# Packing in halves, earlier covariances and unread products in a convolution and whitening kernel

## The chip, the cores and the metric

The kernel runs on one core of one Trainium2 chip. The metric is the device time of that core in microseconds (us), the median of several runs; lower is better. The core has TensorE (matrix products, PE in the profile; its weight loads are PEld), VectorE (DVE), ScalarE (ACT), GpSimd (POOL), SyncE (SP, which here only issues DMAs) and 16 DMA engines, which move data between the large memory (HBM) and the on-chip memory of 128 partitions. TensorE writes into PSUM, a small memory of eight banks, which VectorE and ScalarE empty.

## The reference

The input `x` has 4 images of 64 channels of 256 x 256 numbers in float32. Two layers are computed. The first convolves each channel with a filter of its own over the whole image, and adds `x` times a bias. The filter of a channel is the outer product of two one-dimensional filters, which a small network of sines makes:

```python
k = jnp.einsum('ijk,imk->ijmk', hx, hy)[0]
...
y = jnp.fft.irfft2(u_f * k_f, s=(fft_size, fft_size))[..., :L, :L]
out = y + x * bias[:, None, None]
```

The second layer whitens the 64 channels. The covariance comes from every ninth point, its inverse square root from five Newton-Schulz steps, and all points are multiplied by it:

```python
x1 = jnp.transpose(x, (1, 0, 2, 3)).reshape(B, -1)
x1_s = x1[:, ::STRIDE ** 2]
mean1 = jnp.mean(x1_s, axis=-1, keepdims=True)
xc = x1 - mean1
cov = x1_s @ x1_s.T / x1_s.shape[1] + EPS * jnp.eye(B, dtype=x.dtype)
deconv = _isqrt_newton_schulz(cov, N_ITER)
out = deconv @ xc
```

So no point of the output can be computed before every ninth point of all four convolved images has gone into one 64 x 64 matrix.

## The kernel before

Since a filter is an outer product, the convolution is two products with triangular Toeplitz matrices, one for each direction (L215). The work is cut into 32 steps. A step is one image `n` and one group `g` of 8 channels, and is walked in four groups of two channels, `c` = 0, 2, 4, 6. Steps 0 to 23 take channel groups 0 to 5, each for all four images; steps 24 to 31 take one image after another, with channel groups 6 and 7. Step 25 so ends image 0, step 27 image 1, step 29 image 2, step 31 image 3. "(27,4)" below is step 27, c=4.

`group(first, second)` (L384) computes the first direction of two channels and the second direction of the two channels that stood two groups earlier, in one interleaved stream of TensorE. ScalarE copies the first result (`o`, L399). VectorE adds bias times x to the second and leaves the convolved channels in the x tile (L402). The very first and the last two items are handled by `half_group` (L261).

Three things follow each group. `store(second)` (L410) writes the convolved channels to `y_d` in HBM (L415), and once a step, when the item with c=6 is done, appends nine packing operations to the list `todo`. One such operation (L314) is a predicated copy on VectorE of the points whose index fits the stride of nine, over both halves of the image, into the image's tile `samp[n]`. `pack(time)` (L378) takes operations from `todo` until their estimated cost has used up the time granted. In the last step a part of the channels is packed by TensorE instead (`pack_by_pe`, L289), with selection matrices.

`covariance(n)` (L322) multiplies the packed points of one image with themselves, 58 products of 65 columns on TensorE, and adds the result into `cov` on VectorE (L336). The covariances of images 0 to 2 stand between groups, at (27,4), (29,4) and (31,4); that of image 3 stands after the loop. `whitening` (L447) is a serial chain of small products on TensorE and small operations on VectorE and ScalarE; it contains `spin` products (L424), which nobody reads.

The last pass goes over 32 pieces of 4096 columns. A piece is read back from `y_d` (L352), multiplied by the whitening matrix (L616), shifted and moved out of PSUM by ScalarE (L621) and VectorE (L624), and written from GpSimd's queue (L629). The pieces have no tiles of their own: the list `homes` names, for thirteen pieces in turn, which pool's tile is taken over when its former user is done with it: Toeplitz tiles (t), packed tiles (s), x tiles (i), two spare ones (e). `load_next` issues the next load; the table `early` says after which groups of the loop it is called, and the rest is loaded after the last covariance. All loads and stores of the loop go through SyncE's queue in the order of the program text.

The order on each engine is the order of the program text (`tc.manual_schedule`); an instruction whose input is not ready holds up everything behind it on its engine. The lines that the prediction's steps touch are these:

- the loop over the steps, L553 to L580, with the place of `covariance` at L557
- `pack`, `group`, `store`: L378 to L420; the costs of packing operations: L316
- the end of the loop, L581 to L598: the last two `half_group`s with `pack(1.0)` each, `pack()` for what is left, the multiples of the identity `i15` (L590), `pack_by_pe`, the last covariance, the remaining loads, `whitening`

Of the kernel before, what the change touches and what calls it, by code (L numbers as in the profile page):

```python
# [40 lines left out]
ALU = mybir.AluOpType  # L41
# [3 lines left out]
NB, C, L = 4, 64, 256  # L45
# [3 lines left out]
CG = 8  # L49
# [16 lines left out]
def conv_whiten_kernel(ctx: ExitStack, tc: tile.TileContext, a: dict, out: bass.AP):  # L66
    nc = tc.nc
# [40 lines left out]
    steps = [(g, n) for g in range(C // CG - 2) for n in range(NB)]  # L108
# [10 lines left out]
    ident = const.tile([P, P], F32, tag="ident", name="ident")  # L119
# [33 lines left out]
    for i in range(3):  # L153
        for u in range(2):
# [3 lines left out]
            arg, k, nxt = (scratch[:, 2 + 3 * i + v, half] for v in range(3))  # L158
# [130 lines left out]
    def pack_by_pe(g, n, yt, cs):  # L289

        pk = psA.tile([P, H2, cs.stop - cs.start, NJ], F32, tag="psA", name=f"pk_{cs.start}")
        for s in range(STEP):
            for b in range(H2):
                nj = (L - s + STEP - 1) // STEP
                nc.tensor.matmul(  # L295
                    pk[:, b, :, 0:nj],
                    lhsT=pick[:, (s - b) % STEP, :],
                    rhs=yt[:, cs, b, s : s + STEP * (nj - 1) + 1 : STEP],
                    start=(s == 0 and b == 0),
                    stop=(s == STEP - 1 and b == H2 - 1),  # L300
                    skip_group_check=True,
                )
        dst = samp[n][:, :, :, g * CG + cs.start : g * CG + cs.stop]
        nc.scalar.copy(dst[:, 0], pk[:, 0].rearrange("p c j -> p j c"))  # L304
        copy = nc.vector.tensor_copy if cs.stop == CG else nc.scalar.copy
        copy(dst[:, 1], pk[:, 1].rearrange("p c j -> p j c"))

    def pack_ops(g, n, yt, cs):
        def op(s):
            nj = (L - s + STEP - 1) // STEP  # L310
            src = yt[:, cs, :, s : s + STEP * (nj - 1) + 1 : STEP].rearrange("p c b j -> p b j c")
            dst = samp[n][:, :, 0:nj, g * CG + cs.start : g * CG + cs.stop]
            m = mask[:, n, :, s : s + 1].unsqueeze(3).to_broadcast([P, H2, nj, cs.stop - cs.start])
            nc.vector.copy_predicated(dst, m, src)  # L314

        cost = 0.3 + 1.5e-3 * H2 * NJ * (cs.stop - cs.start)  # L316
        return [(cost, lambda s=s: op(s)) for s in range(STEP)]
# [4 lines left out]
    def covariance(n):  # L322

        pc = psA.tile([P, C + 1], F32, tag="psA", name=f"pc{n}")
        for b in range(H2):
            for j in range(NJ):
                half = slice(C * (j % 2), C * (j % 2 + 1))
                nc.tensor.matmul(  # L328
                    pc[half],
                    lhsT=samp[n][:, b, j, 0:C],  # L330
                    rhs=samp[n][:, b, j, :],
                    start=(b == 0 and j < 2),
                    stop=(b == H2 - 1 and j >= NJ - 2),
                    skip_group_check=True,
                )
        nc.vector.scalar_tensor_tensor(cov, pc, 1.0 / NSAMP, cov, ALU.mult, ALU.add)  # L336
# [4 lines left out]

    homes = [
        {"t": (tpool, "toep"), "s": (spool, "samp"), "i": (xpool, "in"), "e": (epool, "extra")}[k]
        for k in "eetssiistiits"
    ]

    def load_y(i):
# [7 lines left out]
    def load_next():  # L355
        loaded[len(loaded)] = load_y(len(loaded))

    loaded = {}
    todo = []
# [7 lines left out]
    for g in range(1, C // CG):  # L367
        first = 16 * g - 14 if g < C // CG - 1 else 16 * g - 22
        for part in range(8):
            k = first + (part * 12 // 8 if g < C // CG - 2 else part)  # L370
            blocks[k // 4, k % 4 * 2] = (g, part)

    early = {
        (26, 4): 1, (27, 0): 1, (27, 4): 1, (28, 0): 1, (29, 6): 1, (30, 2): 1, (31, 2): 1, (31, 4): 1, (31, 6): 1
    }
    orders = [list(range(L // HP)), list(reversed(range(L // HP)))]

    def pack(time=math.inf):  # L378
        while todo and time > 0:
            cost, op = todo.pop(0)  # L380
            op()
            time -= cost

    def group(first, second):  # L384

        units = []
        g1, n1, c1, x1, o1s1 = first
        g2, n2, c2, x2, o1s2 = second
        for u in range(2):
            job2 = (bank(f"p2_{g2}_{n2}_{c2 + u}"), o1s2[u], toep[g2][:, 1, c2 + u, :])  # L390
            job1 = (bank(f"p1_{g1}_{n1}_{c1 + u}"), x1[:, c1 + u], toep[g1][:, 0, c1 + u, :])
            units.append((job1, job2))

        toeplitz_products(units, orders[0])
        orders.reverse()
        for u in range(2):
            o1 = o1pool.tile([P, H2, L], F32, tag="o1", name=f"o1_{g1}_{n1}_{c1 + u}")
            for to, fr in ((slice(0, HP), slice(HP, P)), (slice(HP, P), slice(0, HP))):
                nc.scalar.copy(o1[to], units[u][0][0][fr])  # L399
            o1s1.append(o1)  # L400
            ch = g2 * CG + c2 + u
            nc.vector.scalar_tensor_tensor(  # L402
                x2[:, c2 + u], x2[:, c2 + u], bias[:, ch : ch + 1], units[u][1][0],
                ALU.mult, ALU.add,
            )

        pack(2.5)
        store(second)

    def store(second):  # L410
        g, n, c, yt, _ = second
        last = (g, n) == steps[-1]
        for b in range(H2):
            row = b * C + g * CG + c
            nc.sync.dma_start(  # L415
                out=y_d[n][row : row + 2, :].rearrange("c (p w) -> p c w", w=L),
                in_=yt[:, c : c + 2, b],
            )
        if last and c == CG // 2 - 2 or not last and c == CG - 2:
            todo.extend(pack_ops(g, n, yt, slice(0, c + 2)))  # L420

    spins = []

    def spin(times):  # L424

        p = psA.tile([P, P], F32, tag="psA", name=f"spin{len(spins)}")
        spins.append(p)
        for _ in range(times):
            nc.tensor.matmul(p, lhsT=ident, rhs=ident, start=True, stop=True)  # L429
# [113 lines left out]
    with tc.manual_schedule(  # L543
        engines={engines.PE, engines.SP, engines.DVE, engines.Activation, engines.Pool}
    ):
        toep = {0: new_toeplitz(0)}

        for f, lo, hi in ((0, 0, 2), (0, 2, 4), (0, 4, 6), (1, 0, 2), (0, 6, 8), (1, 2, 4), (1, 4, 8)):
            for half in range(2):
                load_toeplitz(toep[0], 0, f, half, lo, hi)  # L550
        for c in range(0, CG, 2):
            load_x(x_tiles[1], *steps[1], c)
        for i, (g, n) in enumerate(steps):  # L553
            xt = x_tiles[i % 4]
            for c in range(0, CG, 2):
                item = (g, n, c, xt, [])
                if g == C // CG - 1 and n > 0 and c == 4:  # L557
                    covariance(n - 1)
                if len(pending) == 2:
                    group(item, pending.pop(0))  # L560
                else:
                    half_group(item, 0)
                pending.append(item)
                if i == 0 and c == 6:

                    fold = const.tile([P, C], F32, tag="fold", name="fold")
                    nc.vector.tensor_tensor(fold, ident[:, 0:C], ident[:, C:P], ALU.add)

                    nc.scalar.activation(bf[:, 0:1], samp[0][:, 0, 0, C : C + 1], AF.Sqrt)

                if i + 2 < len(steps):
                    load_x(x_tiles[(i + 2) % 4], *steps[i + 2], c)
                if (i, c) in blocks:
                    tg, part = blocks[i, c]
                    if part == 0:
                        toep[tg] = new_toeplitz(tg)
                    lo = part % 2 * CG // 2
                    load_toeplitz(toep[tg], tg, part // 4, part // 2 % 2, lo, lo + CG // 2)
                for _ in range(early.get((i, c), 0)):
                    load_next()  # L580
        g, n, c, yt, _ = pending[0]  # L581
        for item in pending:
            half_group(item, 1)
            pack(1.0)
            store(item)

        pack()
        i15 = place(2 * C, rows=C).rearrange("p (u c) -> p u c", u=2)
        for u in range(2):
            nc.vector.tensor_scalar(i15[:, u], ident[0:C, 0:C], 1.5, None, ALU.mult)  # L590
        ones = place(P, rows=C)
        nc.gpsimd.memset(ones, 1.0)  # L592
        for lo in range(CG // 2, CG, 2):
            pack_by_pe(g, n, yt, slice(lo, lo + 2))
        covariance(NB - 1)
        while len(loaded) < len(homes):
            load_next()
        W, shift = whitening(i15, ones)  # L598


    halves = [slice(u * C, (u + 1) * C) for u in range(2)]
    for i, (n, q) in enumerate(pieces):
        yt = loaded.pop(i)
# [86 lines left out]
```

## Time and profile before

| | |
|---|---|
| median of 3 runs | 910.22 us (907.89 to 911.49) |
| the profiled execution | 911.4 us, its span 909.6 us |
| TensorE busy | 792.2 us, 87% of the span |
| VectorE busy | 657.6 us, 72% |
| ScalarE busy | 479.8 us, 53% |
| moved by DMA | 285.61 MB, mean 314 GB/s |
| products of L215, share of the chain that ended last | 64% |
| VectorE's L624 in the last pass, share of that chain | 13% |
| one L402 (128x512) | 743 ns, 252 of them |
| one packing copy L314, all channels of a group (128x448) | 972 ns |
| the same for half the channels (128x224) | 610 ns |
| one covariance on TensorE at full clock | 3.71 us |

The span counts from the first to the last instruction of the trace; the execution's time is 1.8 us more. Times in the trace are counted from the start of the span. The page cuts the span into 40 slices of 22.7 us and gives the busy share of each engine in tenths for each. A timeline lists instructions in order of time: start, duration, engine, line, operation, output and input tile, their shapes, how many, and in brackets how long the engine had been idle before and which instruction of which engine ended that. A window row gives the same engine's busy time between two times, with the clock that TensorE was granted (1.00 is full) and what the DMA engines did. A float32 product appears as two records.

The loads for the last pass are issued by SyncE at 510.54, 520.08, 531.15, 542.36, 576.53, 585.05, 603.36, 612.60 and 616.45 us in the loop, and the other four of the thirteen between 624.40 and 637.1.

### The profile page before, as it was taken

The page shows a single profiled execution, that of the slowest core. Times are in us where ns is not written, and L with a number is a line of the kernel's source. Part 1 is how long each engine was busy: PE and PEld are TensorE (multiplying, and loading weights), DVE is VectorE, ACT ScalarE, POOL GpSimd, SP SyncE. Part 2 cuts the span into 40 slices and gives each one's busy share as a digit, 9 for nine tenths or more (in the row PEclk, how much of TensorE's full clock was granted, in tenths as well). Part 3 has the DMA queues.
Part 4 walks back from the last instruction along what each step waited for, and adds up shares of the span by engine and source line. Part 5 has one row for each costly group of instructions (what it writes and reads, how often), then busy time and mean ns, then how long its engine had stood idle before and what let it go on. Part 6 is the DMA issues. An engine that isn't in the chain of part 4 may idle for free.

```text
span 909.6 us, 28286 instructions
## 1 busy us (share of the span) xinstructions
PE 792.2 (87%) x11928; PEld 636.7 (70%) x11928; DVE 657.6 (72%) x882; ACT 479.8 (53%) x798; POOL 31.4 (3%) x71
## 2 busy tenths in 40 slices
PE   8999999999999999999999999999977777775500
PEld 7999999999999999999999999998411111111100
DVE  3368786878687868876787766767699999996500
ACT  2545454545454545555555544541598888885400
POOL 3000000000000000000000000000110000000010
PEclk9999999999999999999999999998999999996655
DMA  4998788797888788878987898879899999999998
GB/s 154 303 305 261 250 243 263 251 276 247 253 262 265 247 255 267 263 249 253 297 282 234 285 400 323 290 253 386 346 383 433 428 432 429 428 433 428 432 430 342
DMA packets 117550, 285.61 MB, mean 314 GB/s; under 512 B 8973, under 2 KB 91312, under 8 KB 109744
## 3 DMA queue, kind: packets, MB, share of 16 engines
q1 hardware_dynamic: 110800, 216.49, 70.1%
q0 software_dynamic: 6336, 67.11, 17.4%
q8 instruction: 95, 1.56, 0.7%
q14 instruction: 31, 0.25, 0.1%
q10 hardware_dynamic: 288, 0.20, 0.1%
HBM read 149.35 MB, written 134.42 MB: 312 GB/s over the span
## 4 chain that ended last, share of the span: by engine, by line
PE 68%; DVE 15%; issue 14%; DMA 1%; POOL 0%; ACT 0%; POOLq 0%; SPq 0%; DVEq 0%; ACTq 0%
PE p L215 64%; DVE yi L624 13%; PE pc L328 2%; PE ph L247 1%; DVE samp L314 1%; PE busy L150 1%; POOL out_dram L629 0%; PE po L616 0%; DMA toep<-g_d 0%; DVE x L284 0%; PE spin L429 0%; PE pm L156 0%; DMA scratch<-in_zw_dram 0%; DMA g_d<-scratch 0%; DVE scratch L163 0%
## 5 line engine op out<-in xcount | busy, mean ns | idle before, releaser
L215 PE MATMUL p<-toep,x 64*64 64x64 f32 (+3 forms) x5040 | 578.5, 284 | 0.0
L215 PE MATMUL p<-toep,o 64*64 64x64 f32 (+3 forms) x5040 | 578.5, 284 | 0.0
L215 PEld LDWEIGHTS p<-toep,x 64*128 64x128 f32 (+1 forms) x5040 | 534.3, 166 | 23.4 <-issue 0.3
L215 PEld LDWEIGHTS p<-toep,o 64*128 64x128 f32 (+1 forms) x5040 | 535.2, 166 | 10.3
L399 ACT COPY o<-p 64x512 f32<-64x512 f32 x504 | 292.2, 580 | 296.0 <-PE p L215 288.5
L314 DVE COPY_PREDICATED samp<-mask,x 128x448 f32<-128x448 int32 (+3 forms) x288 | 281.0, 976 | 6.7
L402 DVE SCALAR_TENSOR_TENSOR x<-x,bias,p 128x512 f32<-128x512 f32 x252 | 177.3, 743 | 138.9 <-PE p L215 138.5
L624 DVE TENSOR_SCALAR yi<-po,shift 64x512 f32<-64x512 f32 x256 | 192.1, 750 | 22.2 <-PE po L616 16.0
L616 PE MATMUL po<-yi,chain 64*64 64x512 f32 x1024 | 152.7, 668 | 59.9 <-DVE yi L624 41.7
L621 ACT ACTIVATE yi<-po,shift 64x512 f32<-64x512 f32 x256 | 174.8, 683 | 38.9 <-PE po L616 31.4
L616 PEld LDWEIGHTS po<-yi,chain 64*64 64x64 f32 x1024 | 35.9, 145 | 175.7 <-DVE yi L624 129.6
L629 POOL DMA_DIRECT2D out_dram<-yi x44 | 23.6, 537 | 256.0 <-DVE yi L624 155.0
L592 POOL MEMSET chain<- 64x128 f32 x1 | 0.2, 198 | 603.0 <-PE ph L247 603.0
L328 PE MATMUL pc<-samp 128*64 128x65 f32 x464 | 17.3, 243 | 2.0 <-ACT samp L304 2.0
L328 PEld LDWEIGHTS pc<-samp 128*64 128x64 f32 x464 | 16.8, 155 | 3.2 <-ACT samp L304 2.2
L150 PE MATMUL busy<-idle 128*128 128x128 f32 x88 | 12.3, 304 | 0.0
L150 PEld LDWEIGHTS busy<-idle 128*128 128x128 f32 x88 | 11.9, 219 | 0.2 <-issue 0.2
L336 DVE SCALAR_TENSOR_TENSOR cov<-pc,cov 128x65 f32<-128x65 f32 x4 | 0.9, 226 | 14.7 <-PE pc L328 14.7
L281 DVE COPY o<-ph 64x256 f32<-64x256 f32 x8 | 3.4, 422 | 9.5 <-PE ph L247 9.4
L281 ACT COPY o<-ph 64x256 f32<-64x256 f32 x8 | 2.9, 366 | 10.4 <-PE ph L247 10.3
L295 PE MATMUL pk<-x,pick 128*128 128x56 f32 (+1 forms) x72 | 8.3, 292 | 0.0
L295 PEld LDWEIGHTS pk<-x,pick 128*128 128x128 f32 x72 | 8.1, 192 | 0.1
(92 smaller groups left out, 84.4 us busy)
## 6 DMA issues: line engine op xcount, KB each, us to landing
x<-in_x_dram SPq DMA_DIRECT2D x128, 512.0 KB, 5.6
y_d<-x SPq DMA_DIRECT2D x256, 256.0 KB, 4.2
yi<-y_d SPq DMA_DIRECT2D x32, 2048.0 KB, 15.1
out_dram<-yi POOLq DMA_DIRECT2D x28, 2048.0 KB, 43.2
out_dram<-yi POOLq DMA_DIRECT2D x16, 512.0 KB, 9.5
toep<-g_d SPq DMA_DIRECT2D x29, 256.0 KB, 6.4
toep<-g_d SPq DMA_DIRECT2D x29, 192.0 KB, 6.4
toep<-g_d SPq DMA_DIRECT2D x6, 128.0 KB, 3.0
```

The lines of the kernel that those rows point to most:

```text
L150: nc.tensor.matmul(p, lhsT=idle[:, 0:P], rhs=idle[:, P : 2 * P], start=True, stop=True)
L215: mm = nc.tensor.matmul(ps[q : q + w, m, HP * k : L], lhsT=src[parts, k // 2, m * P + q : m * P + q + w], rhs=t[parts, : stop : -1] if k e ...
L247: mm = nc.tensor.matmul(ps[m][:, HP * k : L], lhsT=src[parts, k // 2, m * P : (m + 1) * P], rhs=t[parts, : stop : -1] if k else t[parts, : ...
L295: nc.tensor.matmul(pk[:, b, :, 0:nj], lhsT=pick[:, (s - b) % STEP, :], rhs=yt[:, cs, b, s : s + STEP * (nj - 1) + 1 : STEP], start=(s == 0 ...
L314: nc.vector.copy_predicated(dst, m, src)
L328: nc.tensor.matmul(pc[half], lhsT=samp[n][:, b, j, 0:C], rhs=samp[n][:, b, j, :], start=(b == 0 and j < 2), stop=(b == H2 - 1 and j >= NJ ...
L399: nc.scalar.copy(o1[to], units[u][0][0][fr])
L402: nc.vector.scalar_tensor_tensor(x2[:, c2 + u], x2[:, c2 + u], bias[:, ch : ch + 1], units[u][1][0], ALU.mult, ALU.add,)
L616: nc.tensor.matmul(po[u][halves[k]], lhsT=W[halves[u]], rhs=yt[halves[u], cols[k]], start=True, stop=True,)
L621: nc.scalar.activation(yt[halves[0], cols[k]], po[0][halves[k]], AF.Identity, bias=shift[halves[k]])
L624: nc.vector.tensor_scalar(yt[halves[1], cols[k]], po[1][halves[k]], shift[halves[k]], None, ALU.add)
L629: nc.gpsimd.dma_start(out=o[:, end - part : end], in_=yt[:, end - part : end])
```

## The change

```diff
@@ homes
-        for k in "eetssiistiits"
+        for k in "eetssiistitis"
@@ early
-        (26, 4): 1, (27, 0): 1, (27, 4): 1, (28, 0): 1, (29, 6): 1, (30, 2): 1, (31, 2): 1, (31, 4): 1, (31, 6): 1
+        (26, 4): 1, (27, 0): 1, (27, 4): 1, (28, 0): 1, (29, 0): 1, (29, 6): 1, (30, 6): 1, (31, 0): 1, (31, 2): 1, (31, 6): 1
@@ pack
+    credit = [0.0]
+
     def pack(time=math.inf):
-        while todo and time > 0:
+        credit[0] += time
+        while todo and credit[0] > 0:
             cost, op = todo.pop(0)
             op()
-            time -= cost
+            credit[0] -= cost
+        if not todo:
+            credit[0] = min(credit[0], 0.0)
@@ group
-        pack(2.5)
         store(second)
+        pack(2.92)
@@ store
-        last = (g, n) == steps[-1]
+        halves = g >= C // CG - 2
...
-        if last and c == CG // 2 - 2 or not last and c == CG - 2:
-            todo.extend(pack_ops(g, n, yt, slice(0, c + 2)))
+
+        if c == CG - 2 and (g, n) != steps[-1]:
+            todo.extend(pack_ops(g, n, yt, slice(CG // 2 if halves else 0, CG)))
+        elif c == CG // 2 - 2 and halves:
+            todo.extend(pack_ops(g, n, yt, slice(0, CG // 2)))
@@ the loop over the steps
-                if g == C // CG - 1 and n > 0 and c == 4:
+                if g == C // CG - 1 and n > 0 and c == 0:
                     covariance(n - 1)
@@ the end of the loop
-            nc.vector.tensor_scalar(i15[:, u], ident[0:C, 0:C], 1.5, None, ALU.mult)
+            nc.gpsimd.tensor_scalar(i15[:, u], ident[0:C, 0:C], 1.5, None, ALU.mult)
...
             pack_by_pe(g, n, yt, slice(lo, lo + 2))
+        spin(4)
         covariance(NB - 1)
```

In steps 24 to 31 the eight channels of a step are packed in two parts of nine copies each, the first appended when the item with c=2 is done and the second when that with c=6 is done. The store now stands ahead of the packing, so that what it appends can be packed in the same group. The time granted for packing is 2.92 a group instead of 2.5, and what an operation overdraws is carried to the next group; what is not used is dropped when the list is empty. The first three covariances stand at (27,0), (29,0) and (31,0), two groups earlier. Ten loads instead of nine are issued in the loop, the fifth and later ones mostly earlier, and the eleventh and twelfth piece swap their homes (a Toeplitz tile and an x tile). Two operations of `i15` go from VectorE to GpSimd. Four products that nobody reads stand ahead of the last covariance.

## The prediction

> **What bounds the kernel now.** I read the page's slices first.
>
> ```profile
> PE   8999999999999999999999999999977777775500
> ...
> DVE  3368786878687868876787766767699999996500
> ...
> PEclk9999999999999999999999999998999999996655
> DMA  4998788797888788878987898879899999999998
> GB/s 154 303 305 261 250 243 263 251 276 247 253 262 265 247 255 267 263 249 253 297 282 234 285 400 323 290 253 386 346 383 433 428 432 429 428 433 428 432 430 342
> ```
>
> Each digit covers 22.7 us. Up to slice 27 (614 us) TensorE is full: the Toeplitz products of L215 set the pace, at 18.33 us for one step of four groups. After slice 29 (660 us) the DMA engines are full at about 430 GB/s: 19 pieces of 2 MB are still to be read and all 32 written. Between the two lies a serial tail, 614 to 651 us: last half groups, packing by TensorE, the last covariance, whitening, first output (issued at 650.90). Thirteen pieces can be loaded ahead, and in the trace all had landed when the first output was issued, for DMA idles at 649.25 to 652. So the bytes left at that point are fixed, and whatever moves the first output moves the end, one for one. Two places count: a stall of TensorE before 614, and the tail.
>
> The next view is VectorE's timeline around the first covariance.
>
> ```profile
> 506.09 1.41 DVE L402 SCALAR_TENSOR_TENSOR x<-x,bias,p 128x512 f32<-128x512 f32 x2 [3.53 <-PE p L215]
> 507.41 3.09 DVE L314 COPY_PREDICATED samp<-mask,x 128x464 f32<-128x464 int32 x3
> 510.41 1.40 DVE L402 SCALAR_TENSOR_TENSOR x<-x,bias,p 128x512 f32<-128x512 f32 x2
> 511.73 3.02 DVE L314 COPY_PREDICATED samp<-mask,x 128x464 f32<-128x464 int32 x3
> 515.27 1.41 DVE L402 SCALAR_TENSOR_TENSOR x<-x,bias,p 128x512 f32<-128x512 f32 x2 [0.52 <-PE p L215]
> 516.59 2.98 DVE L314 COPY_PREDICATED samp<-mask,x 128x448 f32<-128x448 int32 x3
> 519.50 1.39 DVE L402 SCALAR_TENSOR_TENSOR x<-x,bias,p 128x512 f32<-128x512 f32 x2
> 523.81 0.23 DVE L336 SCALAR_TENSOR_TENSOR cov<-pc,cov 128x65 f32<-128x65 f32 x1 [2.92 <-PE pc L328]
> ```
>
> The covariance of image 0 starts on TensorE at 520.05, ahead of group (step 27, c=4). Counting back, the L402 pairs at 519.50, 515.27, 510.41 and 506.09 belong to groups (27,2), (27,0), (26,6), (26,4). The nine packing copies of image 0's last channel group lie in (26,4), (26,6), (27,0), end at 519.57, and TensorE arrives 0.48 us later. Group (27,2) packs nothing; that one group is the cover.
>
> **The covariances moved by two groups.** I ran through the packing list as the new code fills and empties it. A full copy costs 0.996 in its account, a half copy 0.648. In step 24 three groups are filled by step 23's nine full copies, and only (24,6) appends step 24's first half, behind the last three full ones. From there on 18 half copies a step come in (11.664) against four grants of 2.92 (11.68): what is left over, 0.016 a step, never works off the queue that stands there. So a half appended at (i,2) waits behind four copies of the other half, and is packed in (i,4), five copies, and (i,6), four. For step 25 that is (26,4) and (26,6). The covariance now stands ahead of (27,0), directly behind (26,6). Steps 27 and 29, for the covariances at (29,0) and (31,0), give the same counts.
>
> What TensorE then waits for: VectorE must first do the two L402 of (26,6), which need that group's products, then four copies. No row shows a half copy in the loop; the tail has them, 0.66 us from start to start with 232 elements and 0.645 with 224:
>
> ```profile
> 624.40 0.63 DVE L314 COPY_PREDICATED samp<-mask,x 128x232 f32<-128x232 int32 x1
> ...
> 625.07 0.63 DVE L314 COPY_PREDICATED samp<-mask,x 128x232 f32<-128x232 int32 x1
> ```
>
> On the old times: L402 of (26,4) at 506.09, 1.32 us, five copies 3.3, so L402 of (26,6) at 510.7; plus 1.32, plus four copies of 224 (2.55) gives 514.6. TensorE ends (26,6) at 510.90 (ScalarE's copy of it starts at 510.14, and from such a copy, at 519.29, to the covariance it was 0.76). **Wait: 3.7 us, three times, 11.1 us.** Below, 3.1 each, if L402 of (26,6) starts when its bank is ready (510.1); above, 4.3, if VectorE lags by another half copy. Behind the waiting covariance on TensorE stand all later groups. VectorE's own L336 waits for it too, which costs nothing, since VectorE is idle then. Nothing fills these gaps: the new unread products stand only ahead of the last covariance.
>
> **The clock after such a wait.** The rows to weigh are the last covariance's, beside one in the loop, and the clock in quarter microseconds.
>
> ```profile
> 561.00 3.71 PE L328 MATMUL pc<-samp 128*64 128x65 f32 x116
> ...
> 620.55 8.28 PE L295 MATMUL pk<-x,pick 128*128 128x58 f32 x72
> 630.86 6.20 PE L328 MATMUL pc<-samp 128*64 128x65 f32 x116 [2.04 <-ACT samp L304]
> ```
>
> ```profile
> 629.25:629.50 0.25, 0.00 (x0) 0.92 1.73 594
> 629.50:629.75 0.25, 0.00 (x0) 0.50 1.07 373
> ...
> 636.00:636.25 0.25, 0.25 (x10) 0.50 0.77 328
> 636.25:636.50 0.25, 0.25 (x14) 0.92 1.52 590
> ```
>
> The columns after TensorE's busy time are the granted clock, DMA share and GB/s. After 2.04 us of idling the same 116 products take 6.20 instead of 3.71, at half clock from about 629.45 to 636.27. A second drop runs from 646.5 to 649.9. The edges fit a grid of 3.41 us. The Trainium skill (TensorE: Matmul & The Clock Gate, Part 1: The HAM clock gate) has the same free-running window of about 3.4 us, but lets the clock fall only after at least one idle window. By that rule the gap of 2.04 would have cost nothing, and a gap of 3.7 us holds a whole idle window in only (3.7 - 3.41)/3.41, some 8% of the phases: the clock mostly stays, and the three waits cost 11.1. By the row, 2.04 us suffices, and a window busy for its last 2.0 us (to 632.86) did not bring the clock back. I take the row: after each wait the work runs at half clock until the first window that is nearly all busy ends, 2.5 to 6.8 us later depending on phase. Half of that is lost, 1.2 to 3.4, about 2.2 in the mean; the row itself lost 2.5. **Three times 2.2 is 6.6 us**; bounds 0 (the rule) and 10.
>
> **The tail.** Before, VectorE packed until 630.25 although TensorE's own packing ended at 628.83 (the L295 row), and the covariance started at 630.86. In the new list (31,6) packs step 30's last four half copies; all nine of step 31's first half follow in the tail, two and one behind the half groups' own work and six at the end. On the old times: L402 of (31,6) 614.4 to 615.7, four copies to 618.3, L284 to 620.0, two copies to 621.3, L284 to 622.9, seven copies to 627.5. That is under TensorE's 628.83, so packing by TensorE is late next. Four unread products follow, eight passes at 0.117 (14 take 1.83 in whitening, 0.30 of it the first): to 629.77. The copies out of the last packing bank need about 0.6 and lie beside them. Then the covariance at full clock, 3.75 from its start to L336 (561.00 to 564.75): 633.5 instead of 637.10. **Minus 3.6 us.** If the clock fell anyway it is minus 1.1. The unread products cost some 0.5 over starting at once, and cover the gap in which the clock fell.
>
> **Costed at nothing.** Moving the 1.5 multiples of the identity to GpSimd: two small operations (its 128x128 one took 0.62) at about 620, used at 640.8; bare, they would delay whitening by under 1. Twice as many packing copies in steps 24 to 30: VectorE has 4 x 1.32 + 18 x 0.655 = 17.1 of 18.33 us a step, under TensorE; each bank of PSUM has one group's time to be emptied, so a lag of a few tenths stays hidden. Packing one group sooner in the first 24 steps: it frees x tiles that are loaded two steps ahead; SyncE's waits for it (49.2 us in all) were under TensorE too. Loads sooner and one more of them ahead of the loop's end: SyncE issues each in 0.4 to 0.8 us, and stores queue behind it. At (29,6) and (30,6) it waits for copies of the same group, some 2.6 us, and the stores behind it are late; but no x load comes after step 29, so TensorE doesn't see it. Swapped homes 10 and 11: SyncE takes the Toeplitz tile, free at 620.6, ahead of the x tile, free after 628.83. The thirteenth, freed by the last covariance at 633.5 instead of 637.1, lands within the 13 us to the first output as it did before, so that gains nothing. If they were late, a piece that is used thirteenth would be waited for, far behind the first output.
>
> **Sum**, against the profiled execution (span 909.6, time 911.4): +11.1 + 6.6 - 3.6 = +14.1, span 923.7, time 925.5. That execution lies 1.2 above the median of 910.22; on the median it is 924.3. I take 925.
>
> **Rivals.** (1) The waits come, the clock holds through them, as the skill's rule has it: 911.4 + 11.1 - 3.6 = 918.9. For it: products before and after are dense. Against: both drops in the trace. (2) On the other side: image 0's packing is complete before (26,6), because the queue is shorter there than I count. It decides from one group sooner: TensorE's 4.57 us a group then cover the 3.7, all three waits vanish, and only the tail's gain is left: 911.4 - 3.6 = 907.8. For it: (24,6) alone builds the queue, and without that group's backlog each half would be through in the group that appends it and the next, (26,2) and (26,4). Against: the account of costs leaves no way to work it off. (3) The edits to the tail don't do what they say (clock falls in spite of the unread products) and the waits cost the most: 911.4 + 12.9 + 10 - 1.1 = 933.2.
>
> **How the numbers follow.** Waits with clock loss 0.74, waits without 0.12, no waits 0.10, the costliest 0.04. The likeliest gives 925; within it 919 to 930. Down to 917 it takes in rival 1, and leaves out rival 2 and most of 3. A measurement can't tell 0.5% (4.6 us) from no change: rival 2 is half and half under 905.7 or over it, so faster 0.05, same 0.05, slower 0.90.
>
> **What would show it.** In the new trace: before each of the first three covariances TensorE idle some 3.7 us, released by VectorE's L314; granted clock 0.5 after it; a covariance or the group behind it longer by about 2. The last one at 3.7 instead of 6.2, with no idle ahead of it. First output some 14 us later, and the stretch from there to the end unchanged at 258.7 us. If the first three covariances have no idle ahead, I counted the list wrongly; if that last stretch shrinks, loads mattered where I gave them nothing.

## The result, and the profile after

The changed kernel takes 921.93 us in the median of 6 runs (920.60 to 926.08), the kernel before 909.82 beside it. The ratio is 1.0132, 95% interval 1.0113 to 1.0151: slower by 1.3%, where 925 was forecast, in a range of 917 to 930. The execution with the trace took 921.35, its span is 919.6.

Where the 10.0 us between the two spans lie can be read from five marks that both traces have: ScalarE's copy behind group (2,4), that behind the last group (31,6), the last L336, the issue of the first output, and the end.

| stretch | before | after | difference |
|---|---|---|---|
| start to group (2,4) | 66.59 | 67.24 | +0.65 |
| to the last group of the loop | 547.19 | 560.88 | +13.69 |
| to the last L336 | 23.32 | 19.66 | -3.66 |
| to the first output | 13.80 | 13.01 | -0.79 |
| to the end | 258.70 | 258.81 | +0.11 |

The loop lost 13.7 and the tail won 3.7. The first row is start-up: over the twelve traces of this study that mark lies between 65.9 and 68.8, so one execution can't tell a microsecond there. The row "to the first output" scatters with the clock: it takes 13.0 us in the five traces in which the granted clock stays full from the last L336 to the first output, and 13.8 to 15.5 in the seven in which it falls. The kernel before is one of the seven (0.50 from 646.5 to 649.9, as the prediction read), the changed one of the five.

The first view of the changed kernel is from its list of waits from 25 to 660 us: total, number, longest.

```profile
PEld pc L328 <- issue: 12.2, 3, 4.1
PE pc L328 <- DVE samp L314: 11.1, 3, 3.7
```

Before, TensorE waited for nothing ahead of the three covariances of the loop. The timelines of VectorE and of TensorE around the first one in the changed kernel:

```profile
506.95 1.40 DVE L407 SCALAR_TENSOR_TENSOR x<-x,bias,p 128x512 f32<-128x512 f32 x2 [0.81 <-PE p L215]
508.27 3.27 DVE L314 COPY_PREDICATED samp<-mask,x 128x232 f32<-128x232 int32 x5
511.43 1.39 DVE L407 SCALAR_TENSOR_TENSOR x<-x,bias,p 128x512 f32<-128x512 f32 x2
512.74 2.53 DVE L314 COPY_PREDICATED samp<-mask,x 128x224 f32<-128x224 int32 x4
520.79 0.23 DVE L336 SCALAR_TENSOR_TENSOR cov<-pc,cov 128x65 f32<-128x65 f32 x1 [5.52 <-PE pc L328]
```

```profile
515.42 5.26 PE L328 MATMUL pc<-samp 128*64 128x65 f32 x116 [3.69 <-DVE samp L314]
```

Five copies in one group and four in the next, then the covariance: TensorE had ended its products at 511.73 and waits until VectorE's fourth copy ends, near 515.3. (L407 is the former L402.) The covariance then takes 5.26 instead of 3.71. The window rows, with the granted clock behind TensorE's busy time, show why, and that it is not so each time. The first three are around the first covariance, the last two around the third:

```profile
516.00:516.25 0.25, 0.25 (x15) 0.88 2.12 655
516.25:516.50 0.25, 0.25 (x11) 0.50 0.95 262
...
519.50:519.75 0.25, 0.25 (x13) 0.80 0.91 320
...
604.75:605.00 0.25, 0.00 (x0) 1.00 0.15 53
...
606.75:607.00 0.25, 0.25 (x12) 1.00 0.00 0
```

The clock falls at 516.19 and comes back at 519.60. In the third wait, 602.95 to 606.6, it doesn't fall at all. In the tail the unread products close the gap:

```profile
642.99 1.10 PE L437 MATMUL spin<-ident 128*128 128x128 f32 x8
644.02 3.71 PE L328 MATMUL pc<-samp 128*64 128x65 f32 x116
```

### The profile page after: what moved, and what is told of

Its sections match the earlier page's. It is cut to its first block, busy times and chain, and to the rows that moved or that the text cites. A ratio compares the mean times of both kernels' runs of the same rounds, so it can differ in the third digit from the quotient of the medians.

```text
span 919.6 us, 28365 instructions
## 1 busy us (share of the span) xinstructions
PE 789.4 (86%) x11936; PEld 636.1 (69%) x11936; DVE 678.0 (74%) x943; ACT 479.9 (52%) x798; POOL 32.1 (3%) x73
## 4 chain that ended last, share of the span: by engine, by line
PE 67%; issue 14%; DVE 13%; DMA 4%; POOL 0%; POOLq 0%; ACT 0%; SPq 0%; DVEq 0%
PE p L215 61%; DVE yi L633 10%; DMA out_dram<-yi 2%; PE pc L328 2%; DVE samp L314 2%; DMA yi<-y_d 1%; PE ph L247 1%; DVE x L407 1%; PE pk L295 1%; PE busy L150 1%; POOL out_dram L638 0%; PE spin L437 0%; DMA toep<-g_d 0%; PE pm L156 0%; DMA scratch<-in_zw_dram 0%
## 5 line engine op out<-in xcount | busy, mean ns | idle before, releaser
L314 DVE COPY_PREDICATED samp<-mask,x 128x464 f32<-128x464 int32 (+3 forms) x351 | 296.8, 846 | 9.8 <-DMA y_d<-x 0.2
L407 DVE SCALAR_TENSOR_TENSOR x<-x,bias,p 128x512 f32<-128x512 f32 x252 | 179.1, 743 | 120.1 <-PE p L215 116.5
L625 PE MATMUL po<-yi,chain 64*64 64x512 f32 x1024 | 148.4, 649 | 63.2 <-DVE yi L633 42.2
L336 DVE SCALAR_TENSOR_TENSOR cov<-pc,cov 128x65 f32<-128x65 f32 x4 | 0.9, 227 | 18.6 <-PE pc L328 18.6
```

Of the source, the lines that this page charges most:

```text
L407: nc.vector.scalar_tensor_tensor(x2[:, c2 + u], x2[:, c2 + u], bias[:, ch : ch + 1], units[u][1][0], ALU.mult, ALU.add,)
L625: nc.tensor.matmul(po[u][halves[k]], lhsT=W[halves[u]], rhs=yt[halves[u], cols[k]], start=True, stop=True,)
```

## The experiments

Theory A was that the covariances wait for copies that stand in the queue ahead of them. The rival B was that the place of the covariances, the doubled number of copies or the earlier loads cost the time.

**The queue alone.** One number differs from the changed kernel: in steps 24 to 31 a group may spend 3.2 on packing.

```diff
-        pack(2.92)
+        pack(2.92 if g1 < C // CG - 2 else 3.2)
```

> The changed kernel with one number changed: in steps 24 to 31 a group is granted 3.2 for packing instead of 2.92. By the account the queue is then worked off in steps 24 to 26, the copies of image 0's last half end in (26,4), and those of images 1 and 2 in (28,4) and (30,4), one group before the covariances. Theory A (the covariance waits for copies that stand in its own group): no idle time ahead of the first three covariances, clock at full there, 11.1 + 2.4 us less than the changed kernel's 921.9, so 908.4, and 0.998 of the kernel before or a little less. Rival B (the place of the covariances, the doubled number of copies or the earlier loads cost the time, not the queue): no more than 2 us less than the changed kernel, 920 or over.

907.79 us (10 runs), ratio 0.9973 (0.9958 to 0.9989). VectorE and TensorE at the same place:

```profile
509.38 3.19 DVE L314 COPY_PREDICATED samp<-mask,x 128x224 f32<-128x224 int32 x5
512.47 1.39 DVE L407 SCALAR_TENSOR_TENSOR x<-x,bias,p 128x512 f32<-128x512 f32 x2
513.90 3.29 DVE L314 COPY_PREDICATED samp<-mask,x 128x232 f32<-128x232 int32 x5
```

```profile
512.80 3.71 PE L328 MATMUL pc<-samp 128*64 128x65 f32 x116
```

The copies ahead of the covariance end with image 0 (224 elements: the last five of nine); those behind 512.47 belong to the next image, and TensorE waits for none of them. From group (2,4) to the last group this trace takes 546.99, as before (547.19). All copies, places and loads are as in the changed kernel, so the whole loss of the loop is the queue. B falls. The margin is small: the copies end 0.23 us before the covariance starts.

**One group later instead.**

```diff
-                if g == C // CG - 1 and n > 0 and c == 0:
+                if g == C // CG - 1 and n > 0 and c == 2:
```

with the loads (29,0) and (31,0) moved to (29,2) and (31,2).

> The changed kernel with the first three covariances one group later, at (27,2), (29,2) and (31,2), and the two loads into their packed tiles moved with them, (29,0) to (29,2) and (31,0) to (31,2). The packing queue is as in the changed kernel. Theory A: the group between covers the four copies, no idle time ahead of the covariances, 908.4 as with the larger grant. Rival B (doubled copies or loads): 918 or over. If the copies of the group between delay the covariance as well, idle of up to 1 us each.

912.68 us (21 runs), 1.0029 (1.0019 to 1.0039). The wait for L314 is gone, as expected, but 4 us more are left than expected. In the trace TensorE pauses twice in a stream of products, for 1.93 and 1.06 us, which is 3.0 of the 4.0 us by which the loop is longer than with the grant of 3.2. The first pause:

```profile
523.63 0.27 PE L215 MATMUL p<-toep,o 64*128 64x128 f32 x1 [1.93 <-issue]
```

No releaser is shown. The DMA view of 521.0 to 521.5 has one packet (16 KB) on the queue of instructions, the first since 509.9:

```profile
q1 hardware_dynamic: 186, 0.18, 103.4%
q8 instruction: 1, 0.02, 11.8%
```

From 512.05 to its landing some 10 us later the 2 MB load of (26,4) was under way. Such packets usually come 4 to 9 us apart, but gaps of 11 us also stand in the trace of before (508.6 to 519.7) with no pause behind them. The next kernel leaves that load out (every load moves one place on the list):

> The kernel with the first three covariances at c=2, without the first load for the last pass at (26,4); every load moves to the next place of the list, nine stand in the loop. In that kernel's trace TensorE stood still for 1.93 us behind the covariance of image 0, with no releaser in the trace, and an instruction packet for TensorE's queue had come at 521.3, near the landing of the 2 MB load that was issued at 512.05, 12 us after the packet before it. Theory G (instruction fetch is held up behind such a load): no pause behind that covariance, 2 us less than 912.7 if no other load does the same elsewhere. Rival H (the pause belongs to the covariance's place, through a PSUM bank or VectorE): a pause of 1.9 us in the same place, and 912.7 again.

911.62 us, 1.0006 (0.9994 to 1.0018), where the one with the load had 1.0029. The pause at (27,2) is gone; one of 1.89 us now stands at 603.97, after a packet at 601.6 that came 11 us after its forerunner, with a load issued at 594.56. That speaks against the covariance's place and for an instruction packet that comes late. It doesn't settle it, nor that a load is what holds the packet up: long gaps without a pause exist, the two kernels were not timed side by side, and no run moved the packets alone.

**The clock's part.** Sixteen unread products ahead of each of the first three covariances (`spin(16)`):

> The changed kernel with sixteen unread products ahead of each of the first three covariances (32 passes at 0.117 us, 3.7 us each), which fill the wait and need nothing that is late. Measures the clock's part by itself. Theory A: the wait stays at 3.7 us less what the unread products overlap, so the covariance starts at the same time or at most 0.3 later, but all three take 3.7 at full clock; in the profiled execution that gives back the 2.4 us of clock loss, 1.5 to 3.5 in the median: 918.5 to 920.5. Rival C (the clock is no part of it, the loss lies in the waits alone): 921.9 or up to 1 over.

919.06 us (4 runs), 1.0097 (1.0077 to 1.0117), beside 1.0132: some 3 us. The two intervals just overlap, so it is the trace that carries this reading.

```profile
512.45 3.84 PE L437 MATMUL spin<-ident 128*128 128x128 f32 x32
516.22 3.71 PE L328 MATMUL pc<-samp 128*64 128x65 f32 x116
```

The wait is filled and not shortened, and the covariance takes 3.71. From group (2,4) to the last group the trace needs 558.20, 11.0 more than before: three waits of 3.7. So the clock's part of the changed kernel's 13.69 is 2.6 in its trace.

**Without the unread products of the tail.** The line `spin(4)` is taken out of the changed kernel.

> The changed kernel without the four unread products ahead of the last covariance. Theory A (they hold the clock over the gap in which the last packing bank is copied out): the covariance starts about 0.5 us sooner, after a gap of 0.4 to 0.6 us, and the clock falls as it fell in the kernel before after 0.6 us of idle in the window: 1.7 to 2.7 us lost, so 1.2 to 2.2 us over the changed kernel, 923.1 to 924.1. Rival D (so short a gap doesn't lower the clock): 0.5 us under it, 921.4.

923.15 us (5 runs), 1.0149 (1.0122 to 1.0176); the interval overlaps the changed kernel's. In the trace the last covariance starts after a gap of 0.31 us with the clock full, so the tail to L336 is 0.55 shorter (19.11), as the rival had it. The clock fell later, in whitening, so the stretch from L336 to the first output took 15.51 instead of 13.01; but it fell there in four traces that have the four products, too. The loop's part of the clock was 6.5 in this execution. What these four products are worth in the changed kernel stays open. In the kernel before they are worth something:

> The kernel before with four unread products ahead of the last covariance and nothing else. Theory A (the tail's 3.6 us are packing on VectorE first, 630.25 against 628.83, and clock second): the covariance starts at the same place, 0.9 of the 2.04 us gap are filled, and the clock falls later or not at all; between 0 and 2.5 us less than the kernel before. Rival (the unread products bring the whole 3.6 us): 3 us less or more.

909.24 us (22 runs), 0.9982 (0.9972 to 0.9993). The trace:

```profile
630.53 1.10 PE L429 MATMUL spin<-ident 128*128 128x128 f32 x8
632.71 3.71 PE L328 MATMUL pc<-samp 128*64 128x65 f32 x116 [1.07 <-ACT samp L304]
```

With half the gap filled the clock holds: 20.79 from the last group to L336, 2.53 under the kernel before. The ratio makes it less, 0.6 to 2.5 us; in this trace the clock fell between L336 and the first output, and gave back 0.9 there (14.69 against 13.80). What is left to the changed kernel's 19.66 is 1.13. It is the wait for the last copy of the packing, which the changed kernel does not have; there VectorE is done with its copies at 641.07, ahead of TensorE's own packing.

**The loads alone.** The changed kernel with the old table `early` and the old order of homes:

> The changed kernel with the loads for the last pass issued where the kernel before issued them, nine in the loop, and its order of homes. Theory A (the loads are no part of it, since all thirteen have landed when the first output is written): the changed kernel's 921.9 within 1 us, first output to end 258.7 to 259.1 as in all traces so far. Rival F (the tenth and earlier loads help, or their traffic is part of the loss): 2 us or more off it.

925.83 us (4 runs), 1.0161 (1.0135 to 1.0187): a miss, although this interval overlaps the changed kernel's. Its trace has 260.8 from first output to end where all others have 258.7 to 259.1. The window rows of 657 to 660, just before the first output (662.72 and 660.79), first this kernel, then the changed one; the number before last is the DMA share:

```profile
657.00:660.00 3.00, 2.62 (x22) 1.00 1.00 418
```

```profile
657.00:660.00 3.00, 2.63 (x25) 1.00 0.25 104
```

With the old table the loads are still under way when the first output is written, and the end is 2.0 us later. The last three of the thirteen loads are issued at 648.85, 649.24 and 649.82 here, and at 637.88, 645.14 and 647.82 in the changed kernel. (The two spans differ by 4.0 in all, since the clock's part in the loop is 5.1 in this trace and 2.6 in the other.) This run took back the table and the order of homes together, so it doesn't tell which of the two matters.

**A shorter tail, twice.** On top of the grant of 3.2, VectorE packs two channels more in the last step, TensorE two fewer:

```diff
             store(item)
+            if item[2] == CG - 4:
+                todo.extend(pack_ops(item[0], item[1], item[3], slice(CG // 2, CG // 2 + 2)))
...
-        for lo in range(CG // 2, CG, 2):
+        for lo in range(CG // 2 + 2, CG, 2):
             pack_by_pe(g, n, yt, slice(lo, lo + 2))
-        spin(4)
+        spin(14)
```

> The kernel with the grant of 3.2 and a shorter tail: in the last step VectorE packs two channels more (nine quarter copies, estimated at 0.47 us each from the full and half ones) and TensorE packs only the last two, 36 passes of 0.115 less; fourteen unread products instead of four hold the clock until VectorE is done. Theory A (the tail counts one for one): TensorE's packing ends 4.1 us sooner, VectorE's at about 629.8 on the old times, so the last covariance starts 1.3 us sooner: 906.5, 0.996 of the kernel before. Rival (something else sets the last covariance's start): 907.8 as with the grant alone.

913.61 us, 1.0032 (1.0015 to 1.0049): slower than with the grant alone.

```profile
622.95 7.39 PE L295 MATMUL pk<-x,pick 128*128 128x58 f32 x36 [1.98 <-DVE x L284]
630.15 5.23 PE L437 MATMUL spin<-ident 128*128 128x128 f32 x28
635.31 3.71 PE L328 MATMUL pc<-samp 128*64 128x65 f32 x116
```

With only the last two channels to pack, TensorE waits 1.98 us for them, the clock falls to 0.50 from 624 to 634, and packing and unread products run at half speed. VectorE was done at 628.97, so the unread products, meant as cover, had become the delay. The next kernel places nine ahead of the packing and eight behind it, in place of the fourteen:

> The kernel with the shorter tail, with its fourteen unread products split: nine ahead of TensorE's packing, where TensorE stood idle for 2.1 us and the clock fell, and eight behind it. Theory A (the idle time ahead of the packing let the clock fall, and the unread products behind it then ran at half clock and only delayed the covariance): full clock from the half groups to the last covariance, which starts about 15 us after the half groups began instead of 18.5, so 3.5 us less than that kernel, and 0.5 less than the one with the grant alone: 0.9968 of the kernel before. Rival (the shorter packing itself is slow, or the clock falls elsewhere): 1.000 or over.

907.75 us (10 runs), 0.9969 (0.9958 to 0.9980).

```profile
620.48 2.27 PE L437 MATMUL spin<-ident 128*128 128x128 f32 x18
622.59 4.36 PE L295 MATMUL pk<-x,pick 128*128 128x58 f32 x36
626.77 2.00 PE L437 MATMUL spin<-ident 128*128 128x128 f32 x16
628.98 3.71 PE L328 MATMUL pc<-samp 128*64 128x65 f32 x116 [0.21 <-ACT samp L304]
```

The same packing takes 4.36 instead of 7.39. The grant alone ran beside it:

> The kernel with the grant of 3.2 again, on the same chip as its successor, to compare the two. Theory A: 0.9973 of the kernel before, as it was, and no idle time of TensorE ahead of the first three covariances; a second profile also shows how far the clock's part scatters.

909.45 us (22 runs), 0.9986 (0.9977 to 0.9996), a little behind its first timing. The three waits for L314 are absent again, but the trace has one pause without a releaser of 1.86 us, in the second covariance. So the lowest ratio here belongs to the changed kernel with the grant of 3.2 and the shorter, warm tail: 0.3% under the kernel before and 1.6% under the changed one. Its trace shows the tail's gain (19.02 from the last group to L336 against 19.65), but the interval overlaps that of the grant alone, so between those two the times don't decide.

## Why the prediction was right

**The waits** were right in place, number and size: 3.69, 3.68 and 3.68 against 3.7 forecast, through five and four copies in the two groups ahead. The grant of 3.2 showed that it is the queue. (The covariance of the kernel before starts at 519.98, not at 520.05; that moves the forecast by 0.07.) The grant also brought about what rival 2 describes, a loop without waits, and ran in 907.79 where 907.8 had been worked out. That agreement is in part luck: the sum starts from the profiled execution, 1.2 above the median, and the same kernel took 909.45 the second time.

**The tail** was right: minus 3.66 against minus 3.6. Its parts in the traces, 2.53 from the clock and 1.13 from VectorE's packing, are those stated (2.5 and 1.1).

**The clock's term was too large**: 6.6 in the sum, 2.6 in the profiled execution, about 3 between the ratios with and without the filled waits. In the three traces with unfilled waits it was 2.6, 6.5 and 5.1. The step that failed was "after each wait the work runs at half clock until the first window that is nearly all busy ends", taken from the last covariance. The edges in the new trace, 516.19, 519.60, 560.56 and 563.97, are 1, 12 and 1 times 3.41 us apart. The rows show windows on that grid around the second and the third wait, with TensorE's busy time and the clock granted in the window:

```profile
557.15:560.56 3.41, 0.38 (x4) 1.00 0.94 357
560.56:563.97 3.41, 2.75 (x51) 0.50 1.06 399
...
601.52:604.93 3.41, 1.43 (x14) 1.00 0.16 53
604.93:608.34 3.41, 1.70 (x58) 1.00 0.82 231
```

The windows that ended in a drop were 11% busy here and 23% at the first wait. The two that share the third wait were 42% and 50% busy, and the clock stayed full. The window that brought it back after the second wait was 81% busy, short of "nearly all". So a wait of 3.7 us can cost nothing; here a window edge (604.93) fell in its middle. It did so once: in the three traces the clock fell in eight of nine such waits. No single busy share decides either. A window 38% busy ended in a drop in the kernel with the old loads, and one 45% busy in the kernel without the first load:

```profile
555.63:559.04 3.41, 1.30 (x14) 1.00 0.97 377
```

```profile
601.26:604.67 3.41, 1.52 (x27) 1.00 0.71 233
```

Of the two rules that were weighed, the Trainium skill's (TensorE: Matmul & The Clock Gate, Part 1: at least one idle window) asks for more idleness than these traces do. The row of the last covariance asks for less, since there the clock fell at the end of a window that packing by TensorE had kept 82% busy (2.79 us from 626.04 to 629.45). What is counted no run shows.

**"Gains nothing" for the loads** was half right. The new table and homes bring nothing over the old kernel's end stretch (258.81 against 258.70), but in the changed kernel they are needed: with the old ones the end comes 2.0 us later. I had compared the landing with the first output before, and not asked whether the old places would still be in time once the tail was 3.7 shorter. Whether they are needed without the waits in the loop no run shows.

The sum was +14.1 and the two spans differ by 10.0: minus 4.0 for the clock in the loop, minus 0.8 because the clock fell just ahead of the first output before and not after, plus 0.65 of start-up and small remainders. The time alone would not have told the forecast from rival 1: 921.93 lies about midway between 925 and the 918.9 of waits without clock loss. The traces tell them apart, and show a clock loss between the two.

## What to carry to other kernels

Where a list is filled at a rate equal to the rate at which it is emptied, whatever stands in it at the start stays. Run through the list, operation by operation, before moving a consumer closer to it, and look at the step where the rates change. On an engine that works in program order, leave at least one full group that owes the consumer nothing between the last producer and the consumer. In these runs unread products held the clock where they stood ahead of the idle time; behind it they ran at the low clock themselves and delayed what they were to protect.

## What the hardware showed that I had not expected

- TensorE paused for 1.93, 1.89, 1.86 and 1.06 us within streams of products, with no releaser. In all four an instruction packet of 16 KB had come 2.2 to 2.5 us before TensorE went on, and 7.5 to 11.5 us after its forerunner, with a 2 MB load under way in between. The shortest of these distances is an ordinary one, and the same loads and gaps stand elsewhere without a pause. Three traces also have a pause of 0.7 to 1.1 us at 42 to 51 us, 2.2 to 3.0 us after such a packet, long before the first 2 MB load. What decides is open.
- The same wait of 3.7 us lowered the clock twice and left it full once in one execution; in two others it lowered it each time.
- The stretch from first output to end was 258.7 to 259.1 in eleven of the twelve traces, whatever lay ahead of it.
